# The first four tiles of a routed LoRA kernel in fifteen block products instead of sixteen, with partial sums placed in PSUM by the scalar engine

## The chip, the core and the metric

The kernel runs on one core of one Trainium2 chip. Its time is the device time of one launch in microseconds (us); lower is better. The core has five engines that each work through a list of instructions in order: TensorE (PE; the loading of its weights is shown as PEld), VectorE (DVE), ScalarE (ACT), GpSimd (POOL) and SyncE (SP, which only issues transfers here). An engine that waits for a semaphore holds up everything behind it in its own list. TensorE adds up its results in PSUM; all else lives in SBUF.

## What is computed

```python
W_c  = L0_cond_weights[itok]                       # one 64 x 64 matrix for each of 64 samples
h    = einsum('bct,bcd->bdt', x, W_c)              # x: 64 samples, 64 x 1024
logits = h @ gate_w.T + expert_bias                # 4 experts
pick = one_hot(argmax(logits))
z    = einsum('nh,erh->ner', h, lora_A)            # rank 8 for each expert
delta = einsum('ner,ehr->neh', z, lora_B) summed over the picked expert
out  = x + h @ W_up.T + delta
```

All of it is float32. The kernel changes the order: it multiplies x by one wide matrix first, W = [gate | lora_A | W_up], 1024 x 1060 (4 + 32 + 1024 columns), calls the product U, and applies the 64 x 64 matrices of the samples to U afterwards. Two samples make one tile of 128 rows; there are 32 tiles.

## The kernel before, in words

**Three terms for each product.** A float32 operand is split into a high and a low part: ScalarE copies it to a rounded type (tile names with h: `ah`, `hB`, `hT`, `uh`), VectorE subtracts that from the original (names with l: `al`, `lB`, `lT`, `ul`). A product is high x high + high x low + low x high. ACT first, DVE second, PE third: that is the path of every operand.

**Blocks.** W is cut into 2 x 2 blocks of 512 x 530: B11 and B21 (left columns), B12 and B22 (right columns). A tile of x is cut into two halves of 512 (hf 0 and 1). Two tiles a and b together are a 2 x 2 block matrix A11 = a's half 0, A12 = a's half 1, A21 and A22 those of b. One "product" is one block of A by one block of W: 4 steps of k, 3 terms, 2 PSUM banks, so 24 matmuls. The plain way needs eight products for two tiles. From the third two tiles on (function `seven`), seven are enough, with sums of x (S1 to S4, made on DVE by `sums`) and sums of blocks (T1 to T4).

**Order of work.** Everything goes through `InOrder`, which keeps each engine's list in the order in which the Python program issues it. `run` walks over a list `order` of products and, in each, over k; after step k it runs the hooks that `at(s, k, fn, ...)` put there (k = -1 is ahead of the product). So `at(3, 1, ...)` means: in the lists of the other engines, and of PE for its small matmuls, this stands behind step 1 of product 3. PE's accumulators `c` are three buffers of two banks each (`chain()`); small results go to two banks `o` (`place()`).

**The front of before.** `eight(0)` and `eight(1)` handle tiles 0 and 1, and 2 and 3, in eight products each. B11, B21, B12 and B22 are loaded and split; B12's split shares its buffers with T4's. Later B11 and B12 are loaded a second time (`load_two`) for `sum_t1`, `end_t1` and `make_t2`: T1 = B11 - B12, T2 = T1 + B22, T3 = T2 - B11, T4 = B21 - T2. Where a block from HBM is added, POOL issues a transfer that adds to what the buffer holds (`add_to`).

**Behind the products.** `u_of` or `u_sum` splits a half of U (ACT, then DVE). `apply` is three matmuls with the sample matrices `bd` (split by `split_cond`), `gate` picks the expert (six short instructions on DVE), `turn` transposes the picked z on PE and splits it (ACT, then DVE), `delta` is one matmul with lora_B, `evict` copies to `y` on ACT; after the third part of a tile POOL issues the transfer that adds x to `y`, and SP stores it. `finish` is apply, delta and evict of one of the later parts.

Of the kernel before, what the change touches and what calls it, by code (L numbers as in the profile page):

```python
# [46 lines left out]
def kernel(  # L47
# [24 lines left out]

    nc = tc.nc
# [17 lines left out]
    wh = {b: cpool.tile([P, KH, NB], F32R, name=f"h{b}") for b in BLOCKS}  # L91
    wl = {b: cpool.tile([P, KH, NB], F32R, name=f"l{b}") for b in BLOCKS}

    wh["B12"], wl["B12"] = wh["T4"], wl["T4"]
# [7 lines left out]
    def load_half(i, hf):  # L102
        t = raw[i, hf] = xp.tile([P, KH, P], F32, name="xh", tag="xh")
        (sync if i < 4 else nc.sync).dma_start(t, xt[i, hf])

    def minus_both(t, one, two):
        vector.scalar_tensor_tensor(t, one, -1.0, two, ALU.mult, ALU.subtract)

    def sums(g, name):
        a, b = 2 * g, 2 * g + 1  # L110
        t = tp.tile([P, KH, P], F32, name=name, tag="t")
        if name == "S1":
            f, one, two = minus_both, (b, 0), (b, 1)
        elif name == "S2":
            f, one, two = minus_both, (g, "S1"), (a, 0)
        elif name == "S3":
            f, one, two = vector.tensor_sub, (a, 0), (b, 0)
        else:
            f, one, two = vector.tensor_sub, (a, 1), (g, "S2")
        f(t, raw[one], raw[two])  # L120
        raw[g, name] = t
# [22 lines left out]
    def load_b(q, k):  # L144
        t = raw[q, k] = temp("wraw")
        sync.dma_start(t, part(q, k))
# [5 lines left out]


    def load_two(k):
        load_b("B11", k)
        load_b("B12", k)

    def split_bs(q, ks):

        for k in ks:  # L160
            scalar.copy(wh[q][:, k], raw[q, k])
        for k in ks:
            vector.tensor_sub(wl[q][:, k], raw[q, k], wh[q][:, k].bitcast(F32))

    def add_to(q, k, t, block):
        raw[q, k] = t
        pool.dma_start(t, part(block, k), accum_op=ALU.add)

    def sum_t1(ks):
        for k in ks:  # L170
            t = raw["T1", k] = temp("T1")
            vector.tensor_sub(t, raw["B11", k], raw["B12", k])

    def end_t1(ks):
        split_bs("T1", ks)
        for k in ks:
            add_to("T2", k, raw["T1", k], "B22")

    def make_t1(ks):
        sum_t1(ks)  # L180
        end_t1(ks)

    def make_t2(ks):
        split_bs("T2", ks)
        for k in ks:
            t = raw["T3", k] = raw["B11", k]
            vector.tensor_sub(t, raw["T2", k], t)
        split_bs("T3", ks)
        for k in ks:
            t = raw["T2", k]  # L190
            scalar.mul(t, t, -1.0)
            add_to("T4", k, t, "B21")
# [5 lines left out]
    def part_of_product(g, a, b, first, k, o, n, terms=(0, 1, 2)):  # L198
        h, lo = As[g, a]
        of = (h, wh[b]), (h, wl[b]), (lo, wh[b])  # L200
        for m in terms:
            tensor.matmul(
                o,
                of[m][0][:, k],
                of[m][1][:, k, n],
                start=first and k == 0 and m == 0,
                stop=k == KH - 1 and m == 2,
                skip_group_check=True,
            )
# [4 lines left out]
    def product(g, which, hooks):  # L214

        turns = ((0, 1, 2),) if len(which) == 1 else ((0, 2), (1,))
        for k in range(KH):
            for c, a, b, first in which:
                for terms in turns:
                    for n in BANKS:  # L220
                        part_of_product(g, a, b, first, k, body(c)[:, n], n, terms)
            for kk, fn, *args in hooks:
                if kk == k:
                    fn(*args)

    def product_by_bank(g, places, a, b, hooks):

        for m, (o, n) in enumerate(zip(places, LAST_BANKS)):
            for k in range(KH):
                part_of_product(g, a, b, True, k, o[:, : n.stop - n.start], n)  # L230
# [31 lines left out]
    def u_sum(i, hf, c, t):  # L262
        u_add(i, c, t)
        u_split(i, half(hf), ts["u", i])

# [153 lines left out]
    t = raw["B11", 0] = temp("wraw")  # L419
# [5 lines left out]
    for k in range(2, KH):  # L425
        load_b("B11", k)
    load_halves(sync, 1, slice(0, KH))
    for k in range(KH):
        load_b("B21", k)
    def low(name, k):  # L430
# [5 lines left out]
    for name in ("A11", "A21"):  # L436
        As[0, name] = [ap.tile([P, KH, P], F32R, name=m, tag=m) for m in ("ah", "al")]
    t = raw["B11", 0]
# [52 lines left out]
    def run(g, order, hooks, c):  # L491
        for s, step in enumerate(order):
            step = step if isinstance(step, list) else [step]
            for n, _, _, first in step:
# [5 lines left out]
            product(g, [(c[n], l, r, first) for n, l, r, first in step], hooks[s])  # L500
# [4 lines left out]
    def eight(g):  # L505
        a, b = 2 * g, 2 * g + 1
        h = [[] for _ in range(6 if g == 0 else 8)]
# [4 lines left out]
        def each(s, k, fn, q, ks, *args):  # L512
            for i in ks:
                at(s, k, fn, q, i, *args)

        one, two = (0, 1), (2, 3)
        if g == 0:
            each(0, -1, load_b, "B12", range(KH))
            at(0, 0, keep_warm, 1)
            for n in pieces:  # L520
                at(0, 0, split_b, "B11", 1, n)
            at(0, 0, make_idx)
            for i in range(4):
                at(0, 0, load_cond, i)
            at(0, 0, lambda: pool.dma_start(bias_sb, bias.to_broadcast([P, E])))
            at(0, 0, split_a, g, "A11", STEPS[2])
            each(0, 0, split_b, "B11", (2,))
            at(0, 0, split_a, g, "A21", STEPS[2])
            each(0, 0, split_b, "B11", (3,))
            at(0, 0, split_a, g, "A12")  # L530
            each(0, 0, split_b, "B21", (0,))
            at(0, 1, split_a, g, "A22")
            each(0, 2, split_b, "B21", (1, 2))
            each(0, 3, split_b, "B21", (3,))
            each(1, -1, load_b, "B22", range(KH))
            at(1, 0, load_b3)
            for i in (2, 3):
                at(1, 0, load_half, i, 0)
            each(1, 0, split_b, "B12", (0,))
            each(1, 1, split_b, "B12", (1,))  # L540
            each(1, 2, split_b, "B12", two)
            at(1, 2, split_cond, a)
            at(1, 3, split_cond, b)
            each(1, 3, split_b, "B22", (0,))
            at(2, -1, lambda: u_of(a, 0, c["1"]))
            at(2, 0, load_two, 0)
            at(2, 0, load_two, 1)
            each(2, 0, split_b, "B22", (1,))
            at(2, 2, apply, a, 0)
            at(2, 2, gate, a)  # L550
            at(2, 2, lambda: u_of(b, 0, c["2"]))
            at(2, 3, split_b3, PARTS[0])
            at(3, 1, turn, a)
            for i in (2, 3):
                at(3, 0, load_half, i, 1)
            each(3, 1, split_b, "B22", two)
            at(3, 2, split_a, g + 1, "A11")
            at(3, 3, delta, a, 0)
            at(3, 3, evict, a, 0)
            at(3, 3, split_b3, PARTS[1])  # L560
            at(4, 1, apply, b, 0)
            at(4, 1, gate, b)
            at(4, 2, split_a, g + 1, "A21")
            at(5, -1, lambda: u_of(a, 1, c["3"]))
            at(5, 0, turn, b)
            at(5, 0, sum_t1, one)
            at(5, 0, load_two, 2)
            at(5, 0, load_two, 3)
            at(5, 2, delta, b, 0)
            at(5, 2, evict, b, 0)  # L570
            at(5, 2, end_t1, one)
            at(5, 3, split_a, g + 1, "A12")
            at(5, 3, finish, a, 1)
            order = (
                [("1", "A11", "B11", True), ("2", "A21", "B11", True)],
                [("1", "A12", "B21", False), ("2", "A22", "B21", False)],
                ("3", "A11", "B12", True),
                ("1", "A21", "B12", True),
                ("3", "A12", "B22", False),
                ("1", "A22", "B22", False),  # L580
            )
        else:
            p = a - 1
            at(0, -1, lambda: u_of(p, 1, cs[g - 1]["1"]))
            at(0, 1, finish, p - 1, 2)
            at(0, 1, split_a, g, "A22")
            at(0, 2, make_t1, two)
            at(0, 3, finish, p, 1)
            at(1, 0, finish, p, 2)
            at(1, 1, load_cond, a + 2)  # L590
            at(1, 1, load_cond, b + 2)
            for i in (b + 2, a + 2):
                at(1, 1, load_half, i, 0)
                at(2, 1, load_half, i, 1)
            at(2, 1, make_t2, one)
# [235 lines left out]
```

## Time and profile before

| | |
|---|---|
| median of three runs | 414.69 us (414.54 to 414.86) |
| profiled execution | 415.4 us, of which the span from first to last instruction is 413.6 |
| PE busy | 408.5 us, 99% of the span, 3191 matmuls |
| DVE busy | 285.6 us, 69% |
| ACT busy | 185.0 us, 45% |
| POOL busy | 75.0 us, 18% |
| transfers | 60.99 MB, mean 147 GB/s |
| granted TensorE clock | 0.999 of full speed |

A busy PE row says that matmuls were under way; the share of another engine is an average over the whole run, and a stretch in which that engine is full can hide in it. The 1.8 us between the profiled time and the span lie outside the instructions.

### The profile page before, as it was taken

The numbers are of one execution on the slowest core, as the hardware profiler recorded it, in microseconds if no ns is written. First come the engines' busy times: TensorE is split into PE (matmuls) and PEld (weight loads), VectorE is DVE, ScalarE is ACT, GpSimd is POOL, SyncE is SP. The second block draws the span as 40 slices with busy tenths as digits, with TensorE's granted clock in tenths as the row PEclk, the third lists the DMA queues.
The fourth block names the chain that finished last, engine by engine and source line by source line (L and its number), as shares of the span: only waits on it lengthen the run. The fifth ranks groups of instructions, "written<-read, shape, count | busy, mean of one in ns | idle before, by whom it ended". The sixth has DMA issues, their size and how long they took to land.

```text
span 413.6 us, 8160 instructions
## 1 busy us (share of the span) xinstructions
PE 408.5 (99%) x3191; PEld 407.7 (99%) x3191; DVE 285.6 (69%) x648; ACT 185.0 (45%) x419; POOL 75.0 (18%) x92
## 2 busy tenths in 40 slices
PE   8999999999999999999999999999999999999996
PEld 8999999999999999999999999999999999999995
DVE  5987776876767666676676767666676676766766
ACT  5846734453534445333343534445333344533531
POOL 4304502020020202102020020202102020020000
PEclk9999999999999999999999999999999999999999
DMA  8889964553556435465453555434465443564345
GB/s 276 301 305 224 241 167 98 137 123 99 172 133 177 92 93 143 124 178 135 103 127 98 164 135 159 128 81 138 122 179 135 104 126 94 169 165 124 52 101 178
DMA packets 25830, 60.99 MB, mean 147 GB/s; under 512 B 3328, under 2 KB 5344, under 8 KB 25792
## 3 DMA queue, kind: packets, MB, share of 16 engines
q1 hardware_dynamic: 18112, 40.48, 27.2%
q0 software_dynamic: 6704, 19.21, 27.1%
q10 hardware_dynamic: 976, 0.79, 0.6%
q8 instruction: 25, 0.41, 0.4%
q14 instruction: 13, 0.11, 0.1%
HBM read 43.68 MB, written 16.78 MB: 146 GB/s over the span
## 4 chain that ended last, share of the span: by engine, by line
PE 97%; DMA 1%; issue 0%; POOL 0%; DVE 0%; POOLq 0%
PE c L43 81%; PE o L43 16%; DMA cond_sb<-in_cond_dram 1%; DVE y L43 0%; POOL which L43 0%; POOL condf L43 0%; POOLq L43 0%; POOLq L818 0%
## 5 line engine op out<-in xcount | busy, mean ns | idle before, releaser
L43 PE MATMUL c<-hT,ah 128*128 128x264 f32 x480 | 139.7, 291 | 0.0
L43 PE MATMUL c<-lT,ah 128*128 128x264 f32 x480 | 137.3, 286 | 0.0
L43 PE MATMUL c<-hT,al 128*128 128x264 f32 x480 | 137.1, 286 | 0.0
L43 PE MATMUL c<-hB,ah 128*128 128x264 f32 (+1 forms) x424 | 121.8, 289 | 0.0
L43 PE MATMUL c<-hB,al 128*128 128x264 f32 (+1 forms) x424 | 121.0, 287 | 0.0
L43 PE MATMUL c<-lB,ah 128*128 128x264 f32 (+1 forms) x424 | 119.0, 287 | 0.0
L43 PEld LDWEIGHTS c<-lT,ah 128*128 128x128 f32 x480 | 91.0, 190 | 0.0
L43 PEld LDWEIGHTS c<-hT,ah 128*128 128x128 f32 x480 | 90.9, 189 | 0.0
L43 PEld LDWEIGHTS c<-hT,al 128*128 128x128 f32 x480 | 90.6, 189 | 0.0
L43 POOL DMA_DIRECT2D y<-in_x_dram x31 | 29.3, 945 | 290.3 <-ACT y L43 285.3
L43 PEld LDWEIGHTS c<-hB,ah 128*128 128x128 f32 x424 | 80.7, 190 | 0.3 <-ACT hB L43 0.2
L43 PEld LDWEIGHTS c<-hB,al 128*128 128x128 f32 x424 | 80.7, 190 | 0.0
L43 PEld LDWEIGHTS c<-lB,ah 128*128 128x128 f32 x424 | 79.5, 190 | 0.2 <-issue 0.2
L43 ACT COPY y<-o 128x352 f32<-128x352 f32 (+1 forms) x91 | 40.1, 443 | 58.4 <-PE o L43 55.0
L43 ACT CAST uh<-usum 128x530 fp32r<-128x530 f32 (+4 forms) x44 | 27.1, 616 | 68.4 <-DVE usum L43 68.4
L43 DVE TENSOR_TENSOR al<-S,ah 128x512 fp32r<-128x512 f32 x56 | 38.5, 688 | 24.2 <-ACT ah L43 24.2
L43 DVE TENSOR_TENSOR al<-xh,ah 128x512 fp32r<-128x512 f32 x46 | 31.7, 689 | 30.0 <-ACT ah L43 30.0
L43 PE MATMUL o<-uh,bd 128*128 128x356 f32 (+2 forms) x186 | 44.7, 322 | 0.0
L43 DVE TENSOR_TENSOR ul<-usum,uh 128x530 fp32r<-128x530 f32 (+4 forms) x44 | 30.0, 682 | 18.6 <-ACT uh L43 18.6
L43 ACT CAST zt<-o 96x128 fp32r<-96x128 f32 x31 | 8.1, 262 | 76.0 <-PE o L43 76.0
L43 POOL DMA_INDIRECT wsel<-in_cw_dram,idx x32 | 34.9, 1089 | 10.6 <-issue 5.2
L43 ACT CAST ah<-S 128x512 fp32r<-128x512 f32 x56 | 34.9, 623 | 1.8 <-DVE S L43 1.4
(88 smaller groups left out, 471.3 us busy)
## 6 DMA issues: line engine op xcount, KB each, us to landing
xh<-in_xt_dram SPq DMA_DIRECT2D x60, 256.0 KB
y<-in_x_dram POOLq DMA_DIRECT2D x30, 512.0 KB, 5.6
out_dram<-y SPq DMA_DIRECT2D x30, 512.0 KB
wraw<-in_w_dram SPq DMA_DIRECT2D x23, 265.0 KB
T<-in_w_dram POOLq DMA_DIRECT2D x8, 265.0 KB, 7.3
xx<-in_xt_dram SPq DMA_DIRECT2D x1, 512.0 KB
wsel<-in_cw_dram,idx POOLq DMA_INDIRECT x32, 5.0
y<-in_x_dram SPq DMA_DIRECT2D x1, 512.0 KB
```

The costliest lines, as they stand in the source:

```text
L43: return lambda *a, **k: self.tc.keep_in_program_order(fn(*a, **k))
```

## The change

Tiles 0 to 3 are now handled by one function, `front`, in twelve steps of its `order` (the first and third hold two products, so fourteen), and the fifteenth product is put as an extra second step into `seven(2)`. Tiles 0 and 1 take eight products, tiles 2 and 3 seven. B12 is never split and never loaded alone: T1 = B12 - B11, T3 = B12 - B22, T2 = T1 - B22 and T4 = T2 + B21. The negations are ScalarE's (`start_t1`, `start_t3`), T2's difference is VectorE's, and the additions of B12 and B21 are POOL's adding transfers, of two k each (`add_block`, 530 KB), or one. The raw blocks now lie in buffers that are later T3's and T4's.

Tile 0's right half is written as A11 B11 + A12 B22 + A11 T1. The first term is what step 0 has computed, so ACT copies it out (`keep`, "p0"), and later writes it into a fresh PSUM buffer (`seed`), onto which matmuls add without a start flag. The same is done for tile 1 ("p1") and for tiles 2 and 3 ("p2").

```diff
     def load_b(q, k):
-        t = raw[q, k] = temp("wraw")
+        t = raw[q, k] = before[q][:, k] if q in before else temp("wraw")
         sync.dma_start(t, part(q, k))
...
+    def add_block(q, s, block):
+        i, j = int(block[1]) - 1, int(block[2]) - 1
+        for ks, t in pieces_of(q, s):
+            b = w[j][KH * i + ks.start : KH * i + ks.stop].rearrange("k p n -> p k n")
+            pool.dma_start(t, b, accum_op=ALU.add)
...
+    def start_t1(s):
+        t = before["B11"][:, s]
+        scalar.mul(t, t, -1.0)
+        add_block("T1", s, "B12")
+
+    def start_t3(s):
+        scalar.mul(before["T3"][:, s], before["B22"][:, s], -1.0)
+        add_block("T3", s, "B12")
+
+    def end_t1(s):
+        high_t("T1", s)
+        low_t("T1", s)
...
+    def start_t2(s):
+        for ks, t in pieces_of("T2", s):
+            vector.tensor_sub(t, before["B11"][:, ks], before["B22"][:, ks])
+
+    def end_t2(s):
+        high_t("T2", s)
+        low_t("T2", s)
+        add_block("T2", s, "B21")
...
+    load_half(2, 0)
     load_halves(sync, 1, slice(0, KH))
     for k in range(KH):
         load_b("B21", k)
+    load_half(2, 1)
+    for k in range(KH):
+        load_b("B22", k)
+    for hf in range(2):
+        load_half(3, hf)
...
+        def seed(n, key):
+
+            c[n] = chain()
+            scalar.copy(body(c[n]), ts[key])
...
+        at(0, 3, split_b, "B21", 3)
+        at(1, -1, load_b3)
+        at(1, -1, lambda: keep("p0", c["x1"]))
+        at(1, -1, lambda: keep("p1", c["x2"]))
+        at(1, 0, start_t1, TWOS[0])
+        at(1, 0, split_b, "B22", 0)
+        at(1, 0, split_b, "B22", 1)
+        at(1, 1, split_b, "B22", 2)
+        at(1, 1, split_b, "B22", 3)
+        at(1, 2, split_a, 1, "A12")
+        at(2, -1, lambda: keep("p2", c["y"]))
+        at(2, 0, start_t1, TWOS[1])
+        for m in ("S1", "S2", "S4", "S3"):
+            at(2, 1, sums, 1, m)
+        at(2, 2, split_cond, 0)
+        at(2, 2, split_cond, 1)
+        at(3, -1, lambda: u_of(0, 0, c["x1"]))
+        at(3, -1, lambda: u_of(1, 0, c["x2"]))
+        at(3, 0, split_b3, PARTS[0])
+        at(3, 1, end_t1, TWOS[0])
+        at(3, 1, seed, "x3", "p0")
+        at(3, 2, apply, 0, 0)
+        at(3, 2, gate, 0)
+        at(3, 3, seed, "x4", "p1")
+        at(4, -1, lambda: keep("u2", c["y"]))
+        at(4, 0, end_t1, TWOS[1])
+        at(4, 1, split_a, 1, "S1")
+        at(4, 3, turn, 0)
+        for s in TWOS:
+            at(5, 0, start_t2, s)
+            at(5, 0, start_t3, s)
+        at(5, 1, delta, 0, 0)
+        at(5, 1, evict, 0, 0)
+        at(5, 1, apply, 1, 0)
+        at(5, 1, gate, 1)
+        at(5, 2, end_t2, TWOS[0])
+        at(5, 3, end_t2, TWOS[1])
+        at(6, 2, turn, 1)
+        at(6, 1, split_a, 1, "S4")
+        at(6, 2, split_b3, PARTS[1])
+        at(7, 1, delta, 1, 0)
+        at(7, 1, evict, 1, 0)
+        at(7, -1, lambda: u_of(0, 1, c["x3"]))
+        at(7, 0, split_a, 1, "S2")
+        at(7, 1, end_t3, TWOS[0])
+        at(7, 2, finish, 0, 1)
...
+        at(8, 3, seed, "ya", "p2")
+        at(9, -1, lambda: u_of(1, 1, c["x4"]))
+        at(9, 0, split_a, 1, "A22")
+        at(9, 1, apply, 2, 0)
+        at(9, 1, gate, 2)
+        at(9, 1, sums, 2, "S1")
+        at(9, 1, split_a, 2, "A11")
+        at(9, 3, end_t4, TWOS[0])
+        at(10, -1, lambda: keep("q", c["yb"]))
+        at(10, 0, turn, 2)
+        at(10, 0, sums, 2, "S2")
+        at(10, 3, delta, 2, 0)
...
+        order = (
+            [("x1", x11, "B11", True), ("x2", x21, "B11", True)],
+            ("y", "A11", "B11", True),
+            [("x1", x12, "B21", False), ("x2", x22, "B21", False)],
+            ("y", "A12", "B21", False),
+            ("x3", x12, "B22", False),
+            ("x4", x22, "B22", False),
+            ("x3", x11, "T1", False),
+            ("yb", "S1", "T1", True),
+            ("x4", x21, "T1", False),
+            ("yb", "S4", "B22", False),
+            ("ya", "S2", "T2", False),
+            ("ya", "S3", "T3", False),
+        )
+        run(1, order, h, c)
...
+            if g == 2:
+                order = (order[0], ("ya", (1, "A22"), "T4", False), *order[1:])
```

## The prediction

> **What bounds the kernel now.** I read the page first, then the waits of TensorE, then the chain in order of time, then the windows.
>
> ```profile
> span 413.6 us, 8160 instructions
> PE 408.5 (99%) x3191; PEld 407.7 (99%) x3191; DVE 285.6 (69%) x648; ACT 185.0 (45%) x419; POOL 75.0 (18%) x92
> ...
> PE 97%; DMA 1%; issue 0%; POOL 0%; DVE 0%; POOLq 0%
> ```
>
> ```profile
> PE o L43 <- DVE one L43: 1.0, 1, 1.0
> ```
>
> ```profile
> 20.47 0.49 PE o L43 x3
> ...
> 23.16 0.11 PE o L43
> ...
> 24.75 0.15 PE o L43
> ...
> 31.57 0.64 PE o L43 x4
> ...
> 66.45 2.97 PE c L43 x24
> ```
>
> ```profile
> 7.40:20.00 12.60, 12.60 (x101) 12.43 (x101) 11.77 (x24) 10.95 (x23) 4.98 (x5) 1.00 0.94 334
> 20.00:40.00 20.00, 20.00 (x157) 20.00 (x157) 15.76 (x34) 11.00 (x23) 3.65 (x5) 1.00 0.90 260
> ...
> 100.00:400.00 300.00, 300.00 (x2350) 300.00 (x2349) 202.73 (x462) 126.48 (x292) 47.35 (x47) 1.00 0.49 128
> ```
>
> The chain is 97% PE. The second fence is PE's whole list of waits: one, at the very start. So before loses nothing to waits after 7.4 us, and a matmul taken out is worth its full time. The third fence gives the prices on PE: a product of 24 matmuls 2.97 us (0.124 each), an apply 0.49, a transpose 0.11, a delta 0.15, a finish 0.64. The fourth (columns: PE, PEld, DVE, ACT, POOL busy, granted clock, DMA share, GB/s) says where a new wait can come from: from 7.4 to 20 us DVE is busy 11.77 of 12.60 us and ACT 10.95, with the transfers at 0.94 of their share; in the body DVE is at two thirds. The front, which is rewritten, is the one place without reserve.
>
> **Part 1: the product removed.** Sixteen products become fifteen; the small matmuls (apply, delta, turn) keep their number. Gain: 24 x 0.1235 = 2.96 us, all on the path. In the body (from `seven(3)` on) PE, ACT and DVE do what they did, so nothing else comes from there: S sums with other signs are still one DVE instruction of 0.69.
>
> **Part 2: the waits it adds.** I walk the lists of PE, ACT and DVE through the front with these distances from start to start: ACT 0.54 for 530 columns (three in 1.71 us, the last 0.64), 0.49 from PSUM (18.19 to 18.68), DVE 0.62 (two in 1.33, the last 0.71); 0.605 for 512 columns. The new instructions of 1060 columns have no row: between one instruction of 530 and two; by the slope of the rows 1.07 on ACT, 1.17 on DVE. ACT's copies into PSUM (`seed`, three) have no row either. Nearest are ACT from PSUM (0.49) and to SBUF (0.54): I take 0.54, ends 0.3 and 1.1. A gate on DVE takes 1.3 (59.06 to the next instruction at 60.35).
>
> ```profile
> 11.96 1.71 ACT L43 CAST hB<-wraw 128x530 fp32r<-128x530 f32 x3
> ...
> 18.19 0.59 ACT L43 CAST uh<-c 128x530 fp32r<-128x530 f32 x1
> 18.68 0.64 ACT L43 CAST hB<-wraw 128x530 fp32r<-128x530 f32 x1
> ```
>
> ```profile
> 41.72 1.33 DVE L43 TENSOR_TENSOR wraw<-T,wraw 128x530 f32<-128x530 f32 x2
> ```
>
> PE without waits: step 0 ends at 12.1 (k = 1 starts at 7.37, then 36 matmuls and 0.24 of gaps), step 1 at 15.0, step 2 at 21.0.
>
> *Wait a, start of step 2.* It adds into x1, so it stands behind `keep` p0. SP brings x of tile 2 (256 KB) ahead of B21, 0.7 us later than before; ACT starts B21's k = 0 at 11.6, then has k1, A22, k2, k3 and p0 ends at 15.1. Loss 0.1.
>
> *Wait b, third matmul of the first apply (step 3).* ACT goes on with p1, a negation of 1060, four splits of B22, A12, p2, another negation and four `bd`: 0.49 + 1.07 + 4 x 0.54 + 0.52 + 0.49 + 1.07 + 1.04, so u of tile 0 starts at 21.8. DVE follows: `al` of A12 done at 20.0, four sums for 2.7 us, four `bd` 0.97, then `ul`, done at 24.3. PE is there at 21.05 + 18 x 0.1235 + 0.33 = 23.55. Loss 0.8. The four sums put ahead of `ul` are what makes it late. Before, the sums came at 52 us and were covered.
>
> *Wait c, the first delta (step 5, k = 1).* This is the dear one. T1's second half is: ACT's negation (ends 20.8), POOL's adding transfer of 530 KB (issue 20.85), ACT's split, DVE's split, and only then, on the same DVE list, `al` of S1 and the `zt` that the delta waits for. If the transfer lands at L, the delta can start at L + 1.2 (ACT) + 1.17 + 0.6 + 0.3 (DVE) + semaphores = L + 3.4. Without any wait PE would be there at 15.0 + 5.93 + 2.97 + 0.49 + 2.97 + 0.11 + 1.48 = 29.0. So waits a to c together cost L - 25.6, and at least 1.0, which waits a and b and DVE's list set alone. L:
>
> ```profile
> y<-in_x_dram POOLq DMA_DIRECT2D x30, 512.0 KB, 5.6
> ...
> T<-in_w_dram POOLq DMA_DIRECT2D x8, 265.0 KB, 7.3
> ```
>
> ```profile
> DMA to landing us min/median/max: 5.6/7.3/8.5
> ```
>
> These are the adding transfers of before, from issue to landing. The T rows came in pairs, 530 KB, with SP's loads beside them: the same as here, where SP at 17 to 24 us still brings x of tile 3, lora_B and x of tiles 4 and 5 (SP is not held back: these loads wait for little). The Trainium skill, page "DMA: Bandwidth & Descriptors", section "Anatomy of one DMA — SWDGE (gpsimd) path", gives 2.0 us + bytes / 436e3 for one such DMA: 543 KB would take 3.2 us, by estimate. Then L is 24.1, waits a to c cost their least, 1.0, and the change is faster. The row says 7.3 for half the bytes; a fit without addition and without a neighbour doesn't carry over, and I take the row: L = 20.85 + 7.3 = 28.15. Waits a to c: 2.55. (T1's first half, issued at 16.6, lands at 23.9 by the same row and holds ACT ahead of `seed` x3 for some 0.4 us; that is inside the 2.55, since c ends later.) Ends: 5.6 gives 1.0, 8.5 gives 3.75.
>
> *Wait d, the second delta and the u after it (step 7).* From the first `zt` DVE has T2's difference 2.41, a gate 1.3, T2's low parts 2.41, `al` 0.6, `zt` 0.29: 7.0. PE from the first delta to the second: 0.15 + 0.49 + 1.48 + 2.97 + 0.11 + 1.48 = 6.7. Loss 0.3. Then DVE has lora_B's low part 0.9 and `ul` 0.7 before PE's finish, PE 1.2: again 0.3.
>
> *Wait e, third delta (step 10, k = 3).* ACT's split of A11 waits for the end of step 9 (its buffer), then T4's high part 1.07, DVE's low part 1.17, `zt`: 3.3 us after step 9, PE is there after 3.1. Loss 0.3 with the semaphores.
>
> Other moves cost nothing that I can find. T3 (issue at about 31 and 32) and T4 (37) land 5.6 to 9.8 us later and are needed at 50 and 59. B12 not split (2.2 us of ACT, 2.5 of DVE) and blocks not loaded twice are cover for the rest, already left out of the lists above. The extra step in `seven(2)` finds T4's splits done some 4 us ahead. POOL's later transfers for y queue behind T4's and have 4 us. If the cover at T3 were gone, `hT3` would hold ACT ahead of `seed` ya, at a price of what it is late.
>
> **Sum.** -2.96 + 2.55 + 0.3 + 0.3 + 0.3 = +0.5 us. The profiled execution was 415.4 (span 413.6); the median is 414.69, 0.7 below. The difference carries over to the median: 415.2.
>
> **Rivals.**
> 1. *The transfers land early* (5.6 us or less, as y's do and as the page's price would have it), and waits d or e fall within my errors. Then c sinks to DVE's own limit: -2.96 + 1.0 + 0.9 = -1.1, 413.6; with d and e gone 412.7, and 411.7 if every wait is covered. For it: 5.6 is y's median at twice T's bytes; the front here has one POOL transfer at a time. Against it: that median comes from the body with a DMA share of 0.49, and T's 7.3 from a stretch like this one.
> 2. *Slower: T1's transfers land late and hold ACT, and through ACT the seeds and DVE's whole list.* Place: ACT's `hT1`, first half at step 3, second at step 4. At 8.5 us (T's longest) L = 29.35 and the sum is +1.7, 416.4; at 9.8 (y's longest) L = 30.65, +3.0, 417.7. It decides from L = 28.5 on. For it: the second half queues behind the first, both carry 530 KB in one instruction, and SP sends x of tiles 4 and 5 in the same stretch. Against it: B12 and the second loads of W no longer compete.
> 3. *The change doesn't do what it says:* the page "PSUM — Partial Sum Buffer", section "Summary: rules for kernel authors", wants a seed by ACT to be 0 on this chip. The same page lets a matmul without a start flag add where an earlier matmul has written, which holds for all three buffers here (x1, x2 and y start in them). No trace of before shows it. By either reading PE issues the same matmuls: no change of the time.
>
> **How the numbers follow.** Two versions of this kernel can be told apart from about 0.2%, 0.8 us. My forecast, L between 26.8 and 28.5, gives 413.9 to 415.5 and counts as no change: 0.37. Rival 1 beyond that, below 413.9: 0.27. Rival 2, above 415.5: 0.36. Rival 3 shares the forecast's time. The range leaves out the case that all waits vanish (under 412.8) and transfers beyond y's longest (over 417.3), about one in ten each. The forecast's own range is 413.9 to 415.5.
>
> **What would show it.** Right: PE's waits, empty before, name DVE `ul` near 23.5 us, DVE `zt` near 30 and near 38 to 39, and ACT's list shows `hT1` waiting for a POOL transfer issued near 20.9 that lands near 28; products 24 fewer matmuls; body unchanged. Wrong: no wait on PE in the front and a span near 410.6; or PE waiting for `seed` (ACT `c`) by over 1 us; or T3's transfers named by PE or ACT near 45; or a difference that arises after 70 us.

## The result, and the profile after

The changed kernel takes 418.60 us (median of four runs, 418.21 to 419.11) against 414.77 (four runs, 414.54 to 414.96) for the kernel before: ratio 1.0093, 95% interval 1.0076 to 1.0111. It is slower by 3.8 us, where 0.5 had been forecast. In the profiled executions the span goes from 413.6 to 416.8 us, so 3.2 us more; the rest of the 3.8 is that the profiled execution of before lay 0.6 above its median. It lost that in its first 11 us. This is the 37th matmul of the products, first before, then after:

```profile
10.69 0.28 PE L43 MATMUL c<-hB,ah 128*128 128x264 f32 x1
```

```profile
10.14 0.66 PE L43 MATMUL c<-hB,a 128*128 128x264 f32 x4
```

In three later traces of the instructions of before (runs 9 to 11) it starts at 9.65 to 10.07 us, so I take these 0.5 us for chance of that execution and not for a gain of the change.

The page of the kernel after: the span, the busy time of each engine, and the chain that ended last.

```profile
span 416.8 us, 8078 instructions
PE 408.1 (98%) x3167; PEld 405.9 (97%) x3167; DVE 285.7 (69%) x642; ACT 190.1 (46%) x421; POOL 75.4 (18%) x91
...
PE 86%; DMA 5%; issue 4%; DVE 1%; POOL 1%; ACT 1%; SPq 1%; POOLq 0%; DVEq 0%; ACTq 0%
```

The 24 matmuls are gone (3167 for 3191), yet PE's busy time is nearly what it was (408.1 for 408.5). The chain, 97% PE before, now has DMA, issue, DVE and ACT in it, all of them ahead of 52.8 us; from there on it is PE, up to the last copy on DVE. PE's list of waits (us in total, times, longest) had one row before:

```profile
PE o L43 <- DVE zt L43: 1.8, 2, 1.5
PE o L43 <- DVE ul L43: 1.0, 2, 0.8
PE o L43 <- DVE one L43: 1.0, 1, 1.0
PE o L43 <- DVE bd L43: 0.4, 1, 0.4
```

The timeline of PE places them (start, duration, instruction, idle before it and what ended it):

```profile
23.80 0.43 PE L43 MATMUL o<-uh,bd 128*128 128x356 f32 x1 [0.37 <-DVE bd L43]
25.04 0.43 PE L43 MATMUL o<-ul,bd 128*128 128x356 f32 x1 [0.81 <-DVE ul L43]
32.27 0.42 PE L43 MATMUL o<-b,zt 96*128 96x320 f32 x1 [1.51 <-DVE zt L43]
39.54 0.41 PE L43 MATMUL o<-b,zt 96*128 96x320 f32 x1 [0.32 <-DVE zt L43]
41.20 0.43 PE L43 MATMUL o<-ul,bd 128*128 128x352 f32 x1 [0.20 <-DVE ul L43]
...
52.78 0.41 PE L43 MATMUL o<-b,zt 96*128 96x320 f32 x1
```

The letters are those of the prediction. The first two are wait b, the third is wait c, the next two are wait d, the last is wait e. The idle time in brackets is less than the loss: it counts from the end of the matmul before, and matmuls overlap (one of a product lasts 0.28 us, and the next starts 0.12 us after it); wait e has none at all. From start to start, beyond the usual distance, the third matmul is 1.67 us late and the next one 0.1 more; the last one is 0.29 late. I use this measure below.

Behind wait c stands this list of DVE and, ahead of it, of POOL and ACT, in three timelines:

```profile
21.68 1.20 POOL L43 DMA_DIRECT2D B<-in_w_dram  x1 [4.26 <-ACT bd L43]
```

```profile
23.83 1.07 ACT L43 CAST hT<-B 128x1060 fp32r<-128x1060 f32 x1
25.02 1.22 ACT L43 COPY c<-t 128x530 f32<-128x530 f32 x2
...
28.92 1.08 ACT L43 CAST hT<-B 128x1060 fp32r<-128x1060 f32 x1 [2.06 <-DMA B<-in_w_dram]
```

```profile
21.34 1.42 DVE L43 TENSOR_TENSOR S<-xh,S 128x512 f32<-128x512 f32 x2
22.68 0.69 DVE L43 TENSOR_TENSOR S<-xh 128x512 f32<-128x512 f32 x1
23.28 0.97 DVE L43 TENSOR_TENSOR bd<-wsel,bd 64x64 fp32r<-64x64 f32 x4
24.28 1.33 DVE L43 TENSOR_TENSOR ul<-c,uh 128x530 fp32r<-128x530 f32 x2
...
30.03 1.26 DVE L43 TENSOR_TENSOR lT<-B,hT 128x1060 fp32r<-128x1060 f32 x1 [1.25 <-ACT hT L43]
31.21 0.69 DVE L43 TENSOR_TENSOR al<-S,ah 128x512 fp32r<-128x512 f32 x1
31.92 0.29 DVE L43 TENSOR_TENSOR zt<-o,zt 32x128 fp32r<-32x128 f32 x1
32.24 2.50 DVE L43 TENSOR_TENSOR T<-B,B 128x1060 f32<-128x1060 f32 x3
```

T1's second half is issued at 21.68 and is there at 28.9. ACT (hT) waited 2.06 us for it, DVE (lT) 1.25 for ACT, and the small `zt` stands behind T1's low part on DVE. The `c<-t` row is two of the copies into PSUM, 0.61 us each; nothing on PE waits for them.

The last loss is in no list of waits. In the chain in order of time the body runs without a gap in both kernels. These are the same two places, first of the kernel before, then of the kernel after:

```profile
100.19 2.23 PE c L43 x18
...
403.80 2.96 PE o L43 x24
```

```profile
102.05 2.23 PE c L43 x18
...
406.56 2.97 PE o L43 x24
```

Between them lie 303.61 us before and 304.51 after: the same instructions in the same order take 0.90 us longer. Counted over the last 2640 matmuls it is 337.53 and 338.50 us. The granted clock is 1.00 in both.

### The profile page after: what moved, and what is told of

It is laid out like the page before. It is cut to its first block, busy times and chain, and to the rows that moved or that the text cites. A ratio compares the mean times of both kernels' runs of the same rounds, so it can differ in the third digit from the quotient of the medians.

```text
span 416.8 us, 8078 instructions
## 1 busy us (share of the span) xinstructions
PE 408.1 (98%) x3167; PEld 405.9 (97%) x3167; DVE 285.7 (69%) x642; ACT 190.1 (46%) x421; POOL 75.4 (18%) x91
## 4 chain that ended last, share of the span: by engine, by line
PE 86%; DMA 5%; issue 4%; DVE 1%; POOL 1%; ACT 1%; SPq 1%; POOLq 0%; DVEq 0%; ACTq 0%
PE c L43 71%; PE o L43 15%; DMA B<-in_w_dram 2%; DMA T<-in_w_dram 2%; DMA wraw<-in_w_dram 1%; SPq L43 1%; POOL T L43 1%; DVE al L43 0%; ACT uh L43 0%; DVE lT4a L43 0%; POOL B L43 0%; ACT B L43 0%; DVE ul L43 0%; ACT ah L43 0%; ACT bd L43 0%
## 5 line engine op out<-in xcount | busy, mean ns | idle before, releaser
L43 PE MATMUL c<-hT,ah 128*128 128x264 f32 x488 | 142.2, 291 | 0.0
L43 PE MATMUL c<-hB,ah 128*128 128x264 f32 (+1 forms) x392 | 112.4, 288 | 0.0
L43 PE MATMUL c<-hB,al 128*128 128x264 f32 (+1 forms) x392 | 111.7, 286 | 0.0
L43 PE MATMUL c<-lB,ah 128*128 128x264 f32 (+1 forms) x392 | 110.4, 287 | 0.0
L43 PE MATMUL c<-lT,ah 128*128 128x264 f32 x368 | 105.4, 286 | 0.0
L43 PEld LDWEIGHTS c<-hB,al 128*128 128x128 f32 x392 | 74.4, 190 | 0.0
L43 PEld LDWEIGHTS c<-hB,ah 128*128 128x128 f32 x392 | 74.3, 190 | 0.0
L43 PEld LDWEIGHTS c<-lB,ah 128*128 128x128 f32 x392 | 73.6, 190 | 0.0
L43 PEld LDWEIGHTS c<-lT,ah 128*128 128x128 f32 x368 | 69.8, 190 | 0.0
L43 DVE TENSOR_TENSOR al<-S,ah 128x512 fp32r<-128x512 f32 x60 | 41.3, 688 | 25.8 <-ACT ah L43 25.7
L43 POOL DMA_INDIRECT wsel<-in_cw_dram,idx x32 | 35.2, 1100 | 11.2 <-issue 5.2
```

The costliest lines, as they stand in the source:

```text
L43: return lambda *a, **k: self.tc.keep_in_program_order(fn(*a, **k))
```

## The experiments

The runs came in three groups, each on one chip with its own runs of the kernel before: 1 to 4 (median of before 415.12 us), 5, 6, 9 and 10 (415.02), 7, 8, 11 and 12 (414.81). So a run is compared with the before of its group: what it still loses against that, beside the 3.8 us of the change. Each of these losses is known to about 0.7 us or better. In runs 1 to 8 the theories had in common that the front's waits cause most of the loss; they differed on which link sets them.

**1. The four sums later** (`e1_sums_late`).

```
-        for m in ("S1", "S2", "S4", "S3"):
-            at(2, 1, sums, 1, m)
...
+        for m in ("S1", "S2", "S4", "S3"):
+            at(4, 0, sums, 1, m)
         at(4, 0, end_t1, TWOS[1])
```

> Edit: the four sums of x (S1 to S4 of tiles 2 and 3) leave the place ahead of the first u and stand in VectorE's list behind the first gate. Theory A (one chain): from the landing L of T1's second half VectorE's list is one chain, and the first delta starts at L + 3.4 whatever came before. Then the wait at the first apply falls from 1.7 us to under 0.4, the wait at the first delta grows from 1.7 to about 3.1, and the time stays within 0.4 us of the changed kernel (418.2 to 419.0). Theory B (the waits add up): each wait of TensorE is its own price, and the time falls by 1.4 us to 417.2.

Measured: 418.88 us, ratio 1.0095 [1.0078, 1.0111]. The time is the one that theory A gave, but not for its reason. PE's waits:

```profile
PE o L43 <- DVE zt L43: 2.4, 2, 2.1
PE c L43 <- ACT c L43: 1.4, 1, 1.4
...
PE o L43 <- DVE ul L43: 0.2, 1, 0.2
```

The waits on bd and on the first ul are gone; the row left for ul belongs to wait d. But PE, early at its next product, now waits 1.58 us from start to start for the first seed, which stands behind T1's first half in ACT's list:

```profile
23.92 1.07 ACT L43 CAST hT<-B 128x1060 fp32r<-128x1060 f32 x1 [0.97 <-DMA B<-in_w_dram]
```

And the first delta is 2.26 us late instead of 1.67. T1's second half landed earlier here (ACT splits it at 27.6, which by theory A gives a start at 31.0), but DVE works on the four sums from 27.57 to 30.23 and only then gets to T1's low part; the delta starts at 32.47. So what the move saves at the apply comes back at two places, and only one of them is the sums' doing.

**2. No second operand for T1** (`e2_no_t1_add`). T1's two adding transfers are left out, so T1 is -B11 only.

```
     def start_t1(s):
         t = before["B11"][:, s]
         scalar.mul(t, t, -1.0)
-        add_block("T1", s, "B12")
```

> Edit: the two transfers that add B12 into T1 are left out, so T1 is only the negated B11 and the output is not the reference's; all else is issued as in the changed kernel. Theory A: nothing waits for L any more, VectorE's own list sets the first delta at about 30.5 us instead of 32.3, B22's loads arrive about 1 us earlier, and the time falls by 1.5 to 2 us, to 416.6 to 417.1. Rival C (VectorE's list alone sets the waits and the transfer was hidden beside it): less than 0.4 us.

Measured: 417.02 us, ratio 1.0047 [1.0030, 1.0063], as theory A has it. With nothing to wait for, ACT splits the second half at 26.98 in place of 28.92, and the first delta is 0.33 us late instead of 1.67. The waits on bd and ul stay, and waits a to c together still come to 2.4 us. B22's loads did not arrive earlier, as had been expected (its last split starts at 18.95, in the kernel after at 18.73). The run still loses 1.9 us, so the landing is worth about half of the 3.8.

**3. zt ahead of T1's second half** (`e3_zt_first`).

```
-        at(4, 0, end_t1, TWOS[1])
-        at(4, 1, split_a, 1, "S1")
         at(4, 3, turn, 0)
+        at(4, 3, end_t1, TWOS[1])
+        at(4, 3, split_a, 1, "S1")
```

> Edit: the end of T1's second half (high part, low part) and the split of S1 are moved behind the first turn in all lists, so that zt of the first delta does not stand behind them. Theory A: the wait at the first delta (1.7 us) goes, but T2's difference, the second gate, T2's low parts and the second zt still follow T1's low part on VectorE, so the wait comes back at the second delta, which grows from 0.5 to about 2 us; the time stays within 0.5 us of 418.6. Theory B: the time falls by 1.7 us to 416.9.

Measured: 418.08 us, ratio 1.0072 [1.0055, 1.0089]. It still loses 3.0 us. The first delta no longer waits, but the next turn does (2.0 us from start to start), as the list of waits shows, and something follows that nobody had asked for. In the windows (PE, PEld, DVE, ACT, POOL busy, granted clock, DMA share, GB/s):

```profile
PE o L43 <- ACT ah L43: 1.9, 1, 1.9
```

```profile
34.00:36.00 2.00, 0.15 (x3) 0.09 (x2) 1.79 (x8) 1.85 (x4) 0.26 (x1) 1.00 0.95 153
36.00:37.20 1.20, 1.20 (x11) 1.20 (x12) 1.20 (x2) 0.94 (x2) 0.00 (x0) 1.00 1.16 201
37.20:40.60 3.40, 3.40 (x17) 3.23 (x16) 3.31 (x6) 1.87 (x5) 2.96 (x3) 0.50 1.10 194
40.60:44.00 3.40, 3.40 (x27) 3.40 (x27) 2.65 (x4) 2.83 (x5) 0.00 (x0) 0.99 1.10 195
```

After a stretch of 2 us in which PE did 0.15 us of work, and 1.2 us of full work behind it, it ran at half clock for 3.4 us: 0.22 us from matmul to matmul instead of 0.12, so 17 matmuls where the next 3.4 us have 27. Part of what the reordering saved went there in this execution, at 418.47 us and a mean clock of 0.995; the other three, with clocks of 0.997 to 1.000, took 417.82 to 418.11.

**4. A large reordering** (`e4_reordered`). Against the kernel after, among others:

```
         at(4, 3, turn, 0)
...
         for s in TWOS:
-            at(5, 0, start_t2, s)
             at(5, 0, start_t3, s)
...
+        at(5, 1, end_t1, TWOS[1])
...
+        at(5, 2, start_t2, TWOS[0])
...
+        at(6, 3, start_t2, TWOS[1])
...
+        at(7, 2, end_t2, TWOS[0])
...
+        at(7, 2, end_t2, TWOS[1])
...
+        at(8, 0, end_t3, TWOS[0])
...
+        at(9, 0, end_t3, TWOS[1])
```

> Edit: the same products and the same instructions, other places for the hooks of steps 2 to 11: sums behind the first gate, each zt and each u ahead of the splits that TensorE needs only later (T1's second half, T2, T3, S2, S3, S4, T4), lora_B's second part early. Theory A: the waits of TensorE in the front fall from 5 us to 0.5 to 1.5, the time to 414.3 to 415.3, so about that of the kernel before; what is then left of the gain of 2.96 us is eaten by the slower pace of the body (0.9 us by the profile) and the end (0.4). Theory D (the pace of the body and the end are chance of one execution): the waits fall as in A and the time is 413.0 to 414.0.

Measured: 419.15 us, ratio 1.0104 [1.0087, 1.0121]: a miss by 4 us.

```profile
PE o L43 <- DVE z L43: 1.5, 1, 1.5
PE o L43 <- ACT bd L43: 1.1, 1, 1.1
...
PE c L43 <- ACT c L43: 0.9, 1, 0.9
PE o L43 <- DVE bd L43: 0.7, 1, 0.7
```

The waits on ul and zt that I aimed at are gone, the one on the seed is not. The splits of T2 and T3, pushed back to 39 to 47 us, are now ahead of tile 2's bd (ACT) and of its gate (DVE), and PE waits there. ACT's list has no gap from 38.8 to 48.0 us here, so what is pushed into it makes something else late.

**5. T1's negations, and with them its transfers, one place earlier** (`e5_negate_early`).

```
+        at(0, 0, start_t1, TWOS[0])
         at(0, 0, split_a, 1, "A11")
...
-        at(1, 0, start_t1, TWOS[0])
+        at(1, 0, start_t1, TWOS[1])
...
-        at(2, 0, start_t1, TWOS[1])
```

> The kernel after the change, with T1's two negations (ACT) and so its two adding transfers (POOL) one place earlier each: the first at the end of ACT's list in step 0, the second where the first stood. Nothing else moves. Theory A (the landing L of T1's second half sets the waits a to c, as L - 25.6 down to a least of about 1): L comes from 28.9 to about 23.5, the wait of the first delta falls from 1.7 us to under 0.4, the waits of the first apply on ul stay (the four sums still stand ahead of it), time 415.9 to 416.6. Theory B (DVE's list is the bound by itself, whenever T1 lands): the wait moves but the sum stays, 417.8 to 418.6.

Measured: 417.37 us, ratio 1.0051 [1.0034, 1.0068], between the two theories. The issue came 5.6 us earlier, at 16.03, but ACT splits the data at 27.17, only 1.7 us earlier, and not because it waits for them. From DVE's and ACT's timelines:

```profile
20.95 0.69 DVE L43 TENSOR_TENSOR S<-xh 128x512 f32<-128x512 f32 x1 [0.34 <-DMA xh<-in_xt_dram]
```

```profile
25.35 1.22 ACT L43 COPY c<-t 128x530 f32<-128x530 f32 x2 [1.14 <-DVE ul L43]
...
27.17 1.08 ACT L43 CAST hT<-B 128x1060 fp32r<-128x1060 f32 x1
```

The sums wait for x of tile 3, bd is 1.22 us late (the second matmul of the apply, 0.64 in the kernel after), and the seeds, which go to the PSUM buffers that ul reads, hold ACT until ul is done. So here the lists and not L set the split, which is theory B's reason; the wait c has shrunk to 0.31. The DMA view has a landing for one of T1's halves, the first:

```profile
B<-in_w_dram POOLq DMA_DIRECT2D x2, 530.0 KB, 9.8
```

It took 9.8 us, with B22 and x of tile 3 on their way at the same time. When the second landed, this trace does not show; run 6, which issues it at nearly the same time, does.

**6. That, and the sums in DVE's gap** (`e6_order2`). x of tile 3 is loaded ahead of B22, so the sums can stand where DVE waited 1.5 us for B22.

```
     load_half(2, 1)
+    for hf in range(2):
+        load_half(3, hf)
     for k in range(KH):
         load_b("B22", k)
...
+        at(1, 0, split_a, 1, "A12")
+        at(1, 0, start_t1, TWOS[1])
+        for m in ("S1", "S2", "S4", "S3"):
+            at(1, 0, sums, 1, m)
```

> As the run with the early negations, and in addition: x of tile 3 is loaded ahead of B22, so that the four sums can stand in DVE's gap before B22's low parts (14 to 17 us) instead of ahead of ul; the split of A12 and of B21's last k stand differently around ACT's keeps; the split of S4 and the second finish stand one place later. Theory A (all that is left of the front's loss is the order of the lists): PE's waits in the front fall from 5.0 to under 1.8 us, time 414.6 to 415.6. Theory B (the lists are full and a wait only moves to another place): 416 or more.

Measured: 416.17 us, ratio 1.0030 [1.0017, 1.0043], by its number on theory B's side; it still loses 1.2 us. bd and ul are in time. Two waits over 0.3 us are left: the seed (0.8 us) and zt (1.3), the latter because T1's second half, issued at 16.3, lands at 27.1:

```profile
27.08 1.08 ACT L43 CAST hT<-B 128x1060 fp32r<-128x1060 f32 x1 [1.62 <-DMA B<-in_w_dram]
```

That is 10.8 us from issue to landing, against 7.2. An issue 5.4 us earlier than in the kernel after brought the data 1.8 us earlier: while the loads of B22 and x run, L gains little by an earlier issue.

**7. Fewer neighbours for T1's transfer** (`e7_x45_late`). The kernel after, with one move:

```
-        (sync if i < 6 else nc.sync).dma_start(t, xt[i, hf])
+        (sync if i < 4 else pool if i < 6 else nc.sync).dma_start(t, xt[i, hf])
...
+        for i in (4, 5):
+            for hf in range(2):
+                at(5, 0, load_half, i, hf)
```

> The kernel after the change with one thing moved: the four loads of x of tiles 4 and 5 (1 MB) go from SP's queue, where they run at 19 to 25 us beside T1's second adding transfer, to POOL's queue behind T3's transfers (after 32 us). Theory A (the length of T1's transfer, 7.2 us, comes from its neighbours on the DMA engines): the second half lands at least 1.5 us earlier than 28.9, the wait of the first delta falls from 1.7 us by as much, time 416.6 to 417.6. Theory B (an adding transfer of 530 KB takes its 7 us by itself): it lands at 28.5 or later, time 418.3 or more. In either case the waits on bd and ul of the first apply (1.7 us) stay.

Measured: 416.47 us, ratio 1.0041 [1.0026, 1.0057], slightly better than theory A. In ACT's timeline:

```profile
26.77 1.08 ACT L43 CAST hT<-B 128x1060 fp32r<-128x1060 f32 x1 [0.84 <-DMA B<-in_w_dram]
```

The transfer issued at 20.75 is there at 26.8, 6.0 us later instead of 7.2; the issue itself came 0.9 earlier. The first delta is late by 0.43 us, and the waits on bd and ul stay, as expected. The run loses 1.7 us, so this one group of loads, moved alone, returns 2.2; that is as much as run 2 returned, within the noise.

How much of it is the neighbours? The issue is not: runs 1, 3 and 4 have it at 20.5 to 20.7 too. The length seems to be. SP issues five loads of x between 18 and 24 us in the kernel after and in run 3, and the transfer took 7.2 and 8.5 us; two in runs 1 and 4, 6.9 and 6.8; one here, 6.0. With one trace each, and 1.2 us between two of the same kind, the order speaks for the neighbours, but the size is not settled.

**8. Both together** (`e8_order3`). The reordering of 6 with the move of 7, the first seed and the first gate ahead of T1's first split.

> The last reordered kernel, in which T1's second transfer was issued at 16.3 us and landed only at 27.1, with three more moves: x of tiles 4 and 5 on POOL's queue behind T3's transfers; the first seed ahead of T1's first split on ACT; the first gate ahead of T1's first low part on DVE. Theory A: T1's second half lands near 24 to 25 us, both waits that were left there (0.8 on the seed, 1.3 on zt) go, PE's waits in the front are under 0.9 us, time 413.8 to 414.6: below the kernel before the change. Theory B (one of the transfers that are now later, x of 4 and 5 or T4's, becomes the new wait at 45 to 52 us, or DVE's list alone holds the delta): 415.2 or more.

Measured: 414.88 us, ratio 1.0004 [0.9995, 1.0012], between the two theories: the loss is gone, a gain is not shown. The seed's wait is gone and ul is 0.4 us late; zt is still 1.2 us late, since T1's second half still lands at 26.5: with the loads of B22 and x beside it, it takes 10.3 us from its issue at 16.1. My 24 to 25 was wrong.

**9. to 11. Where the tiles lie.** Three kernels with the instructions of before: a shift of the small tiles by 32 bytes (`b1_shift32`), W's tiles in the order of after (`b2_w_order`), and all of it (`b3_all_places`).

```
+    cpool.tile([P, 8], F32, name="pad")
```

```
+    for m in "hB11 lB11 hB21 lB21 hT1 lT1 hB22 lB22 hT2 lT2 lT3 hT3 hT4 lT4".split():
+        (wh if m[0] == "h" else wl)[m[1:]] = cpool.tile([P, KH, NB], F32R, name=m)
```

> The kernel before the change, with an unused tile of 32 bytes per partition placed behind the blocks of W, so that all tiles allocated later (the split x, u, the routing weights) lie 32 bytes further on, at the places that they have in the kernel after. The same instructions. Theory P (the slower pace of the body comes from where those tiles lie): the last 2640 matmuls take 338.5 us instead of 337.5, time 0.9 above before. Theory Q (from where the blocks of W lie, or from something else in the change): 337.5, time as before within 0.3.

> The kernel before the change, with the tiles of the blocks of W allocated in the order that they have in the kernel after (high and low part of a block side by side), all other tiles where they were. The same instructions. Theory P: the last 2640 matmuls take 337.5 us, time as before within 0.3. Theory Q: 338.5, time 0.9 above before. If neither this run nor the one with the shift is slower, the pace comes from something else, such as the state of the chip between executions.

> The kernel before the change with its tiles where the kernel after has them: blocks of W in its order, T4's low part as two tiles, the rest 32 bytes further on. The same instructions. The shift alone gave 337.97 us for the last 2640 matmuls, the order of W alone 337.62, the kernel before 337.53, the kernel after 338.50. Theory P: the two together give 338.3 to 338.6. Theory Q: no more than the sum of the two, 338.1.

Measured: 415.31 us, ratio 1.0006 [0.9997, 1.0015]; 415.08 us, 1.0003 [0.9995, 1.0012]; 415.65 us, 1.0018 [1.0010, 1.0027]. The last 2640 matmuls take 337.97, 337.62 and 338.54 us. Neither part alone makes the longer body (the shift makes not quite half of it); all places together give the body of the kernel after to 0.04 us, with the instructions of before, and cost 0.8 us of time. From the chain of the third:

```profile
99.42 2.23 PE c L43 x18
...
403.94 2.97 PE o L43 x24
```

That is 304.52 us between the two places, against 303.61 before and 304.51 after.

**12. The best order with the places of before** (`e9_order3_places`): the instructions of 8, W's tiles at the addresses of the kernel before and 96 unused bytes behind them.

```
     for q in ("B11", "B21", "T1", "B22", "T2"):
...
+        wh[q] = parts_of("h", q)
+    raw_at("B22", "hT3")
+    raw_at("T3", "hT4")
+    for q in ("B11", "B21", "T1", "B22", "T2"):
+        wl[q] = parts_of("l", q)
+    raw_at("B11", "lT3")
+    raw_at("T2", "lT4b")
+    cpool.tile([P, 24], F32, name="pad")
```

> The same instructions as the third reordered kernel, but the tiles lie in SBUF as in the kernel before the change: the high parts of W first and the low parts behind, at the same addresses as there, and an unused tile of 96 bytes behind them, so that x, u and the routing weights lie as before modulo 128 bytes. Theory P (the pace of the body depends on where the operands lie): the last 2640 matmuls take 337.5 to 337.7 us instead of 338.5, time 0.8 to 1.0 below the third reordered kernel. Theory Q (it comes from something else in the change): 338.5, the same time within 0.3.

Measured: 413.99 us (413.21 to 414.66), ratio 0.9981 [0.9971, 0.9992]: the one kernel here that beats the kernel before. It is 0.9 us below run 8, as theory P has it, with the same instructions. Its chain has 303.47 us between the two places, and the 2640 matmuls take 337.37:

```profile
98.46 2.20 PE c L43 x18
...
401.93 2.95 PE o L43 x24
```

What is left in its front is mainly one wait, 1.25 us from start to start (wait e is there too, with 0.3):

```profile
PE o L43 <- DVE zt L43: 1.1, 1, 1.1
```

```profile
26.50 1.08 ACT L43 CAST hT<-B 128x1060 fp32r<-128x1060 f32 x1 [0.84 <-DMA B<-in_w_dram]
```

All its stops together, with the restarts behind them, are 1.8 us more than before has, its end is 0.2 longer and its body 0.2 shorter: -2.96 + 1.8 + 0.2 - 0.2 = -1.2 us by the trace, -0.8 (-1.2 to -0.3) by the times.

## Why the prediction was wrong

The chain of waits was right; three terms of the sum were not. The waits of the front came to 5.4 us where the sum had 3.45, wait b most of all. The body, put at nothing, took 0.97 us longer, and so did the end, 0.4. "Measured" is the lateness from start to start in the trace of after, with the 0.1 us that PE loses again on the matmul behind a wait; for the product removed it is 24 times the usual distance.

| step of the sum | predicted, us | measured, us |
|---|---|---|
| product removed | -2.96 | -2.96 |
| wait a | 0.1 | 0.0 |
| wait b | 0.8 | 2.0 |
| wait c, its part beyond a and b | 1.65 | 1.8 |
| wait d | 0.6 | 1.0 |
| wait e | 0.3 | 0.6 |
| start, up to the 37th matmul of the products (chance) | not in the sum | -0.5 |
| body | 0 | 0.97 |
| behind the last matmul | 0 | 0.4 |
| sum | 0.5 | 3.3 (spans: 3.2) |

Without the chance of the start the sum is 3.8, the difference of the medians.

*Wait b was sized wrong.* The step said that ul is done at 24.3 and PE there at 23.55. ul was done near 25.0: B22's last k came at 18.7, later than the list assumed, so `al` of A12 and the four sums behind it were 0.7 later; PE was there 0.4 earlier. (The step's own sums come to 21.9 us for u of tile 0 and 23.6 for PE, not 21.8 and 23.55; that changes nothing.) The step also left out that bd, not only ul, stands behind the sums: the second matmul of the apply was 0.64 late, the third another 1.08. Part of this is chance: in four traces of the same loads (runs 1, 3, 4 and 7) B22's last k was there by 17.6 to 17.8, in run 2 at 18.9, and in run 3, whose lists are the same up to here, wait b was 1.1 us.

*Wait c was right in mechanism and nearly in size.* L was 28.9 for 28.15: the transfer took 7.2 us from issue (7.3 taken), and the issue was 0.8 late, most of it for the reason above. That the lengths agree so well is luck: the row was of transfers of half the bytes, and runs 1, 3 and 4 have 6.8 to 8.5 us for this one. The formula L - 25.6 gives 3.3 for the waits a to c together; they came to 3.8. Nor was SP free, as the step had it: two of the four loads of x for tiles 4 and 5 started only at 22.8 and 23.4 us, beside the transfer. Of the two sources weighed there, the row held and the Trainium skill's price in "DMA: Bandwidth & Descriptors", section "Anatomy of one DMA — SWDGE (gpsimd) path" (3.2 us for this size, by estimate) did not: even with the x loads out of its way the transfer took 6.0. But the formula treats L as the only free term above a floor of 1.0. The floor was too low: in run 2, where nothing waits for a landing, waits a to c still come to 2.4 us. DVE's list makes it, which is busy for 11.2 of the 13 us from 20 to 33 us, and through ul the seeds and ACT's list (runs 1 and 5).

*Waits d and e*, 1.6 us for 0.9, were priced by the list alone. The restart behind each wait, about 0.1 us, was left out everywhere; with six stops it makes 0.6 us.

*"Body unchanged" was the step that failed outright.* The argument was that PE, ACT and DVE do what they did, which put nothing for where their operands lie. They do, and the body is still 0.97 us longer, by the places of the operands in SBUF (runs 9 to 12). The prediction named "a difference that arises after 70 us" as something that would make it wrong; it did arise.

*The tail*: from the last matmul to the end it is 4.62 us after and 4.20 before. Kernels with the new front have 4.3 to 4.7, those with the old one 4.1 to 4.2. What causes it stays open.

*Rivals.* The slower one named T1's landing and its decision point L = 28.5; L passed it, so it is the nearest to what happened, but by its own formula it gives 1.2 to 1.3 us for L = 28.9, less than half of the loss, and no seed held PE. The rival of early landing is refuted. The copies into PSUM worked as seeds, 0.61 us each (0.54 taken from start to start), in the changed kernel without a wait of PE. T3's transfers are named by no wait of PE, as predicted.

## What to carry to other kernels

When a front has two engines and the DMA nearly full at once, removing work from a third buys only what those lists allow: price the new waits by walking all the lists with measured landings, and count the restart of PE after each. Here, moving one instruction out of a nearly full list's way made another late (runs 1, 3 and 4); what helped was to take work that isn't urgent off the crowded resource (x of tiles 4 and 5, 2.2 us) and to put work into a gap that the trace shows (the sums, run 6). Look at the start of both traces before comparing spans: half a microsecond of chance lay there. An unchanged loop isn't unchanged when its tiles move: compare two distant marks in the chain of both kernels before arguing about the rest.

## What was not expected of the hardware

- The start-to-start time of matmuls depends on where the operands lie in SBUF: 337.37 to 338.54 us for the same 2640 matmuls, 0.35%, with ten kernels that share the places of after within 0.07 us of each other. Which bits of the address matter is open. By a count over these matmuls, a shift of 32 bytes mostly slowed the small ones (148.9 to 149.9 ns in the mean) and the order of W's tiles did the same (150.1), while it made those of the products a little faster (124.4 to 124.2 ns); with all places together the products are slower too (124.65).
- PE's clock fell to 0.50 for 3.4 us soon after a single stretch of about 2 us with little work (run 3), but not in the profiled execution of run 1 after a wait of 2.26 us. Two of the four executions of the kernel after, and two of run 1's, have a mean clock of 0.993 or 0.994, where none of the kernel before in the three groups is under 0.997; they took 0.4 to 0.5 us longer in the mean than the other two. No trace of them was kept, so their cause is not shown. By the two at full clock the change loses 3.6 us.
- An adding transfer of 530 KB took 6.0 us from issue to landing beside one load of x, 6.8 to 8.5 beside two to five, and 9.8 to 10.8 beside loads of W (runs 6, 8 and 12).
